# Last stage of a four-layer kernel written in turns: MLP, top-k choice and experts in an order given by hand, with more of the work on ScalarE

## The chip, the core and the metric

The kernel runs on one core of a Trainium2 chip. A core has engines that each work through their own queue of instructions in order: TensorE (PE in the profile; its weight loads are PEld), VectorE (DVE), ScalarE (ACT), GpSimd (POOL), and SyncE (SP), which issues the DMA transfers here. Semaphores make an instruction wait for another engine's result. Matrix products go into PSUM, eight banks of 128 partitions by 512 floats; everything else lies in SBUF. The metric is the device time of one execution in microseconds (us).

## The reference

Eight blocks follow one another, each as `x = x + layernorm(block(layernorm(x)))`, on x of 16 sequences, 256 positions and 128 features in float32. The change lies in the last pieces of this. The seventh block ends in an MLP with a square (all names as in the reference):

```
xa = xa + a_mlp_scale * (square(relu(rms_norm(xa) @ a_fc_w)) @ a_proj_w)
x  = x + layernorm(xa)
```

The eighth block is a mixture of experts in which each of 8 experts chooses its tokens in each sequence. The reference takes k = 2 * t / 8 tokens, which is 64 of 256:

```
probs = softmax(x @ gate_w)                # per token, over 8 experts
g, m  = top_k(probs transposed, k)         # per expert, its 64 tokens
xin   = x[m]
h     = gelu(xin @ w1) @ w2                # 128 -> 512 -> 128, an expert each
out   = zeros.at[m].add(g * h)             # then to bfloat16
x     = x + layernorm(out)
```

## The kernel before, in words

The 16 sequences are kept as 8 groups g of two (`NG`); a group is a tile of 128 partitions by 4 x 128 floats (`NT` = 4 blocks of tokens). `program` runs the stages one after the other. Each stage opens its own pool of working tiles and its own split of the PSUM banks (`LAST_BANKS`: six banks "s" and two "sum" in the last one). A tile asked for under a tag takes the next of that tag's buffers (`bufs`) and waits until the earlier content has been read.

Stages are written as Python generators. A generator emits some instructions and yields. `turns` takes a list of (start turn, generator) and, turn by turn, advances each generator that has begun by one step, in the order of the list; one that is late may make up to three steps. Thus the order in which the source emits instructions is that of the turns. In the stages ahead of the last one `turns` runs inside `k.tc.manual_schedule()`, and each engine's queue then has just this order. In `stage_last` it does not: there the framework's planner sets each engine's order, from its own estimates of durations and with the order of the source as priority.

The last stage (`stage_last`) has three kinds of generators.

`last(g)`, for each group: the MLP in `l3_mlp`, the residual in `residual`, then `choice_gate`. In the MLP, POOL squares the input (L290), VectorE sums (L292), POOL takes the power -1/2 (L245), VectorE multiplies (L298), TensorE transposes (L306) and a copy brings the result to SBUF as `nT`. Four matmuls with `afc` give the hidden layer; ScalarE does relu (L1438) and VectorE multiplies relu by the PSUM value, which is the square (L1439). Sixteen matmuls with `aproj` follow, and VectorE adds to xm (L1444). All matmuls go through the helper at L317. A layer norm is `stats` (VectorE L255 and L257, POOL L244 and L245) and `normed` (four VectorE instructions, L264). `choice_gate` norms x into `xn` (tile name exn), transposes it, multiplies by the gate's weights and takes the softmax over 8 experts into `probs`.

`selection(q)`, for each of four quarters q of four sequences: 32 rows (4 sequences by 8 experts) of 256 probabilities; eight rounds of `max` and `match_replace` on VectorE mark the 64 largest, and three small matmuls rank them into slot numbers.

`pair_of(q, pair)`, 16 of these: for two experts and four sequences, VectorE builds one-hot matrices (`hot`) and POOL the same weighted by the probability (`back`). TensorE gathers the tokens with `hot` into one bank (`xin`), transposes `back` (L1730) into `put`, runs the two experts' w1 and w2, and adds the result back to token positions through `put` into the two banks `sums`. After the fourth pair of a quarter the sums are normed, added to x and stored by DMA.

`copy` at L237 and L239 is a helper that gives every second copy to VectorE and every other to ScalarE. The start turns before are these:

```
    items = [(2 * g if g < 6 else 4 * g - 8, last(g)) for g in range(NG)]
    for q in range(4):
        items.append(((15, 19, 23, 36)[q], selection(q)))
        items += [(21 + 12 * q + 3 * pair, pair_of(q, pair)) for pair in range(4)]
```

The weights of the experts and the gate are issued on SP when the previous stage has ended, 17 transfers that follow one another.

## Time and profile before

| | us |
|---|---|
| median of 3 runs | 3017.48 (3016.08 to 3022.56) |
| the profiled execution, its own time | 3016.38 |
| its span, first to last instruction | 3014.7 |
| busy in the span: TensorE, VectorE, ScalarE, POOL | 2753.9, 1999.3, 1607.1, 1010.7 |
| first instruction of the last stage (POOL, L290, group 0) | starts 2685.78 |
| last matmul of the last stage | ends 3002.76 |

Times inside the profile count from the start of the span. A line of a group has the source line, the engine, the operation, output and inputs with partitions x elements, and how often; then busy time in us and the mean of one in ns; then the engine's idle time just before and which instruction ended it. A float32 matmul of the source appears as two records. A line of a stretch has the start and end, the length, the busy time of each engine with its number of instructions, then the clock that was granted to TensorE (1.00 is full), the DMA share and GB/s. A line of a wait has the waiting engine and tile, the releaser, the total in us, how often, and the longest. A line of the chain has the start, the length and the work. Matmul ends are modelled and overlap the next one's start a little, so lengths of matmul groups are read here from start to start.

### The profile page before, as it was taken

What the parts mean: (1) busy time and instruction counts of PE and PEld (TensorE: products, weight loads), DVE (VectorE), ACT (ScalarE), POOL (GpSimd) and SP (SyncE); (2) the same over time, 40 slices, a digit from 0 to 9 for tenths busy, and PEclk for the clock granted to TensorE, in tenths of its full rate; (3) what the DMA queues carried; (4) which work ended last, traced back from release to release, by engine and by line L of the source; (5) the groups of instructions that cost most, each with busy time, mean ns of one, the idle gap of its engine ahead of it and who ended that gap; (6) DMA issues with size and microseconds to landing.
All of it is one profiled execution on the core that took longest, in us unless ns stands there. A gap on an engine that the chain in (4) does not pass through costs nothing.

```text
span 3014.7 us, 59480 instructions
## 1 busy us (share of the span) xinstructions
PE 2753.9 (91%) x23674; PEld 1882.7 (62%) x23674; DVE 1999.3 (66%) x5462; ACT 1607.1 (53%) x3376; POOL 1010.7 (34%) x1368
## 2 busy tenths in 40 slices
PE   8979999999997799999959997899999699978898
PEld 4647766777666588888743443566666344436897
DVE  5667465574657989999776774565765577638542
ACT  6745556555563567767615665344443377642332
POOL 3553333333335100000044554322222466553332
PEclk9989999999998899999979998899999799988999
DMA  4000000000000000000110000000000000010000
GB/s 114 11 1 2 1 2 2 1 2 1 2 5 33 1 16 8 8 8 8 31 50 1 1 1 1 1 1 1 1 1 2 1 1 1 1 57 1 1 15 15
DMA packets 29150, 31.30 MB, mean 10 GB/s; under 512 B 7292, under 2 KB 20156, under 8 KB 28732
## 3 DMA queue, kind: packets, MB, share of 16 engines
q1 hardware_dynamic: 28872, 27.49, 3.1%
q8 instruction: 187, 3.06, 0.4%
q14 instruction: 91, 0.75, 0.1%
HBM read 23.29 MB, written 4.19 MB: 9 GB/s over the span
## 4 chain that ended last, share of the span: by engine, by line
PE 48%; DVE 9%; ACT 6%; POOL 3%; issue 2%; DMA 0%; POOLq 0%; SPq 0%; ACTq 0%; DVEq 0%
PE ps_s L317 30%; PE ps_o L317 7%; PE ps_mm L317 6%; ACT at_e L472 1%; ACT lg L1129 1%; PE ps_s L306 1%; POOL ln_rs L245 1%; ACT meT L1136 1%; PE ps_sum L317 1%; ACT mdisp L1036 1%; DVE ln_st L255 1%; ACT lg L1009 1%; PE ps_s L506 1%; PE ps_t L1134 1%; DVE at_nm L440 1%
## 5 line engine op out<-in xcount | busy, mean ns | idle before, releaser
L244 POOL TENSOR_SCALAR ln_rs<-ln_mv 128x4 f32<-128x4 f32 x192 | 40.2, 209 | 849.5 <-DVE ln_mv L257 827.8
L440 DVE TENSOR_REDUCE at_nm<-ps_s 128x2 f32<-128x512 f32 (+1 forms) x384 | 238.0, 681 | 122.3 <-PE ps_s L317 122.3
L472 ACT ACTIVATE at_e<-ps_s 128x512 f32<-128x512 f32 x384 | 198.1, 604 | 92.5 <-PE ps_s L317 90.3
L1391 DVE TENSOR_TENSOR scan<-ps_s,lm 128x384 f32<-128x384 f32 x256 | 124.6, 548 | 143.3 <-PE ps_s L317 143.0
L478 POOL TENSOR_SCALAR_AFFINE_SELECT at_e<-at_e 128x1024 f32<-128x1024 f32 (+1 forms) x96 | 135.1, 1408 | 215.5 <-ACT at_e L472 215.2
L245 POOL TENSOR_TENSOR ln_rs<-ln_rs,mhalf 128x4 f32<-128x4 f32 x192 | 196.0, 1021 | 15.7
L854 DVE TENSOR_REDUCE l_max<-ps_s 128x3 f32<-128x384 f32 x256 | 124.0, 547 | 64.1 <-PE ps_s L317 64.1
L317 PE MATMUL ps_o<-my,meT 128*128 128x129 f32 x1024 | 144.4, 288 | 18.8 <-ACT mgot L1148 16.1
L317 PEld LDWEIGHTS ps_s<-l_w,mlp_h 128*128 128x128 f32 x1280 | 149.4, 192 | 19.0 <-issue 15.3
L317 PE MATMUL ps_s<-l1f_phi,mxT 128*128 128x256 f32 x512 | 141.5, 399 | 16.8 <-DVE mpart L1010 16.8
L317 PEld LDWEIGHTS ps_o<-my,meT 128*128 128x128 f32 x1024 | 128.0, 195 | 37.0 <-ACT mgot L1148 22.5
L317 PE MATMUL ps_s<-km,qT 32*128 32x512 f32 x768 | 139.8, 659 | 11.9 <-POOL km L364 10.5
L317 PE MATMUL ps_s<-l_w,mlp_h 128*128 128x128 f32 x1280 | 150.2, 275 | 0.3
L317 PE MATMUL ps_s<-qm,kT 32*128 32x512 f32 x768 | 143.8, 655 | 5.2 <-DVE at_nm L440 5.0
L904 POOL TENSOR_SCALAR_AFFINE_SELECT e<-e 128x512 f32<-128x512 f32 x128 | 78.5, 634 | 178.5 <-ACT e L901 178.5
L317 PE MATMUL ps_o<-at_e,at_vm 128*32 128x128 f32 (+1 forms) x2048 | 122.7, 336 | 15.2 <-ACT at_oT L502 15.2
L317 PE MATMUL ps_mm<-mdisp,mxn 128*128 128x128 f32 x1024 | 125.3, 279 | 5.0 <-DVE mdisp L1048 4.9
L901 ACT ACTIVATE e<-ps_s 128x384 f32<-128x384 f32 x256 | 105.6, 513 | 39.7 <-PE ps_s L317 39.6
L317 PEld LDWEIGHTS ps_mm<-mdisp,mxn 128*128 128x128 f32 x1024 | 121.8, 195 | 7.9 <-DVE mdisp L1048 6.6
L317 PE MATMUL ps_s<-xT,l_w 128*128 128x512 f32 x256 | 119.3, 596 | 2.7 <-ACT mlp_h L789 2.7
L1368 ACT COPY BT<-ps_s 128x512 f32<-128x512 f32 x64 | 37.5, 586 | 154.6 <-PE ps_s L317 154.6
L317 PEld LDWEIGHTS <-b_ident 128*128 128x128 bf16 x656 | 51.4, 98 | 109.3 <-issue 99.5
(427 smaller groups left out, 7098.4 us busy)
## 6 DMA issues: line engine op xcount, KB each, us to landing
mw<-in_l1fw SPq DMA_DIRECT2D x16, 256.0 KB, 2.7
moe_w<-in_moe SPq DMA_DIRECT2D x16, 256.0 KB, 5.3
l_w<-in_l SPq DMA_DIRECT2D x10, 256.0 KB, 3.3
x<-in_x SPq DMA_DIRECT2D x8, 256.0 KB, 4.3
xs<-x SPq DMA_DIRECT2D x8, 256.0 KB, 2.0
slT<-xs SPq DMA_DIRECT2D x8, 256.0 KB, 2.8
out<-x SPq DMA_DIRECT2D x8, 256.0 KB, 2.3
l1f_phi<-in_l1f SPq DMA_DIRECT2D x1, 1024.0 KB, 4.9
```

The costliest lines, as they stand in the source:

```text
L244: g.tensor_scalar(out, in_, scale, eps, ALU.mult, ALU.add)
L245: g.tensor_tensor(out, out, self.mhalf[:, :n], ALU.pow)
L255: v.bn_stats(out=st[:, k, :], in_=src[:, k, :])
L317: self.nc.tensor.matmul(out, lhsT=lhsT, rhs=rhs, start=start, stop=stop, skip_group_check=True)
L440: v_.tensor_reduce(nm[:, t, r, vs], s, AX.X, ALU.max, negate=True)
L472: nc.scalar.activation(e[:, r], s, AF.Exp)
L478: nc.gpsimd.affine_select(at, at, [[0, 4], [0, n], [1, P]], ALU.is_ge, 0.0, base=0, channel_multiplier=-1)
L854: v.tensor_reduce(mx[:, b, :, h, 16], s, AX.X, ALU.max, negate=True)
L901: nc.scalar.activation(e[:, h].rearrange("p j n -> p (j n)"), s[:, : 3 * P], AF.Exp)
L904: nc.gpsimd.affine_select(e[:, :, j, :], e[:, :, j, :], [[0, 4], [1, P]], ALU.is_ge, 0.0, base=0, channel_multiplier=-1)
L1368: nc.scalar.copy(s, ps)
L1391: v.tensor_tensor(m, s[:, : SEQ + P], lm[:, SCAN_HEADS[4 * (t // 2) + 2 * i + hh], :], ALU.mult)
```

## The change

The last stage is put inside `manual_schedule`, with new start turns: the MLP and gate of groups 0 to 5 start at turns 0, 1, 3, 5, 7 and 9, those of groups 6 and 7 at 19 and 21; the selections at 19, 25, 33 and 42; and a pair of experts starts at every second turn from 25. In the list the latest pairs come first, then the selections, then the groups.

`l3_mlp` and `choice_gate` go; their work is written out in `last(g)`, cut into more steps with idle turns after the statistics. The square is a second ScalarE activation in place of VectorE's multiply. All copies out of PSUM are ScalarE's, with one more of them for the MLP's result, which is then added in SBUF. The norm into `xn` is done by four ScalarE activations with scale and bias; POOL makes the bias. The probabilities are written by VectorE without POOL's copies.

In `pair_of` the one-hot matrices are built in twos, a step ahead of their use; the gathered tokens have a PSUM bank of their own ("xin", so five remain for "s"); two sequences' transposed `back` share one bank and one copy of 512 columns. At the end of a quarter both halves are copied and both have their statistics taken before either is normed. More buffers are given to `hot`, `back` and `mlp_h`.

```diff
@@ -32,7 +32,7 @@
 BANKS = {"mm": 2, "s": 2, "o": 2, "t": 2}
 MAMBA_BANKS = {"s": 6, "o": 2, "mm": "s", "t": "s"}
-LAST_BANKS = {"s": 6, "sum": 2, "mm": "s", "t": "s"}
+LAST_BANKS = {"s": 5, "sum": 2, "xin": 1, "mm": "s", "t": "s"}
 ONE_RING = {"s": 8, "mm": "s", "t": "s"}
 RING_BANKS = {"s": 7, "o": 1, "mm": "s", "t": "s"}
 NEG = -(2.0**100)
@@ -1424,26 +1424,6 @@
-def l3_mlp(k, x, fc, proj, bufs=3):
...
@@ -1630,32 +1610,6 @@
-def choice_gate(k, x, g, w, xn, probs):
...
@@ -1667,12 +1621,78 @@
     iota = k.c["iota"].rearrange("p (e c) -> p e c", e=2)
     slots, sums = {}, {}
+    def normed(out, src, mv, rs):
+
+        nb = k.t([P, NT], "ln_nb", 3)
+        nc.gpsimd.tensor_scalar(nb, mv[:, :, 0], -1.0, None, ALU.mult)
+        nc.gpsimd.tensor_tensor(nb, nb, rs, ALU.mult)
+        yield from idle(2)
+        for t in range(NT):
+            nc.scalar.activation(
+                out[:, t, :], src[:, t, :], AF.Identity, bias=nb[:, t : t + 1], scale=rs[:, t : t + 1]
+            )
+
     def last(g):
-        yield from l3_mlp(k, xm[g], w["afc"], w["aproj"], 2)
-        yield
-        yield from k.residual(x[g], xm[g])
-        yield
-        yield from choice_gate(k, x, g, w, xn, probs)
+        xg = xm[g]
+        sq = k.t([P, NT, D], "rms_sq", 2)
+        nc.gpsimd.tensor_tensor(sq, xg, xg, ALU.mult)
+        yield
+        ss = k.t([P, NT], "rms_ss", 3)
+        v.tensor_reduce(ss, sq, AX.X, ALU.add)
+        rs = k.t([P, NT], "rms_rs", 3)
+        k.rsqrt(rs, ss, 1.0 / D, RMS_EPS)
+        yield from idle(2)
+        n = k.t([P, NT, D], "n", 2)
+        v.tensor_tensor(n, xg, bc(rs, 2, D), ALU.mult)
+        yield
+        ps = k.transposed_ps(n)
+        nT = k.t([P, GT], "nT", 2)
+        nc.scalar.copy(nT, ps)
+        yield
+        h = k.t([P, 4, GT], "mlp_h", 4)
+        for i in range(4):
+            ps = k.ps("s")
+            k.mm(ps, w["afc"][:, i * P : (i + 1) * P], nT)
+            nc.scalar.activation(h[:, i, :], ps, AF.Relu)
+            nc.scalar.activation(h[:, i, :], h[:, i, :], AF.Square)
+            if i % 2:
+                yield
+        ps = k.tokens_ps(h, w["aproj"].rearrange("p (c n) -> p c n", c=4))
+        y = k.t([P, NT, D], "ln_y", 3)
+        nc.scalar.copy(y, ps)
+        yield
+        v.tensor_tensor(y, y, xg, ALU.add)
+        mv, rs = k.stats(y)
+        yield from idle(2)
+        k.normed(y, y, mv, rs)
+        nc.gpsimd.tensor_tensor(x[g], x[g], y, ALU.add)
+        yield
+        mv, rs = k.stats(x[g])
+        yield from normed(xn[g], x[g], mv, rs)
+        yield
+        ps = k.transposed_ps(xn[g])
+        xT = k.t([P, GT], "xT", 2)
+        nc.scalar.copy(xT, ps)
+        yield
+
+
+        ps = k.ps("s")
+        for t in range(NT):
+            k.mm(ps[:, t * ne : (t + 1) * ne], xT[:, t * P : (t + 1) * P], w["gate"])
+        p = k.t([P, NT, ne], "p", 3)
+        nc.scalar.copy(p, ps[:, : NT * ne].rearrange("p (t e) -> p t e", t=NT))
+        yield
+        m = k.t([P, NT], "pm", 3)
+        v.tensor_reduce(m, p, AX.X, ALU.max)
+        v.tensor_tensor(p, p, bc(m, 2, ne), ALU.subtract)
+        nc.scalar.activation(p, p, AF.Exp)
+        yield
+        v.tensor_reduce(m, p, AX.X, ALU.add)
+        v.reciprocal(m, m)
+        for b in range(2):
+            at, ts = (2 * g + b) * ne, slice(2 * b, 2 * b + 2)
+            v.tensor_tensor(probs[:, :, at : at + ne], p[:, ts, :], bc(m[:, ts], 2, ne), ALU.mult)
+        yield
     def selection(q):
@@ -1681,22 +1701,25 @@
         for t in range(2):
             nc.tensor.transpose(ps[:rows, t * P : (t + 1) * P], probs[:, t, rows * q : rows * (q + 1)], ident)
         cur = k.t([rows, SEQ], "top", 2)
-        v.tensor_copy(cur, ps[:rows, :SEQ])
+        nc.scalar.copy(cur, ps[:rows, :SEQ])
+        yield
         for n in range(cap // 8):
             best = k.t([rows, 8], "best", 2)
             v.max(out=best, in_=cur)
             nxt = k.t([rows, SEQ], "top", 2)
             v.match_replace(out=nxt, in_to_replace=best, in_values=cur, imm_value=-1.0)
             cur = nxt
-            if n % 2:
+            if n in (2, 5):
                 yield
         chosen = k.t([rows, SEQ], "chosen", 1)
         v.tensor_scalar(chosen, cur, 0.0, None, ALU.is_lt)
+        yield
         ps = k.ps("s")
         for t in range(2):
             nc.tensor.transpose(ps[:, t * rows : (t + 1) * rows], chosen[:, t * P : (t + 1) * P], ident[:rows, :rows])
         mk = k.t([P, 2, rows], "mk", 2)
-        v.tensor_copy(mk, ps[:, : 2 * rows].rearrange("p (t r) -> p t r", t=2))
+        nc.scalar.copy(mk, ps[:, : 2 * rows].rearrange("p (t r) -> p t r", t=2))
+        yield
         rank = k.ps("s")[:, : 2 * rows].rearrange("p (t r) -> p t r", t=2)
         k.mm(rank[:, 0, :], k.c["before"], mk[:, 0, :])
@@ -1709,31 +1732,41 @@
     def pair_of(q, pair):
-        put = k.t([P, nb, SEQ], "put", 4)
-        y = k.t([P, nb, D], "ey", 3)
-        xinT = k.t([P, nb, P], "xinT", 2)
-        xin = k.ps("s").rearrange("p (b c) -> p b c", b=nb)
-        for i in range(nb):
+        def one_hot(i):
             b, r = nb * q + i, i * ne + 2 * pair
-            hot = k.t([P, 2, P], "hot", 4)
+            hot = k.t([P, 2, P], "hot", 6)
             by_expert = hot.rearrange("p t (e c) -> p t e c", e=2)
             v.tensor_tensor(by_expert, bc(iota, 1, 2), bc(slots[q][:, :, r : r + 2], 3, cap), ALU.is_equal)
-            back = k.t([P, 2, P], "back", 4)
+
+            back = k.t([P, 2, P], "back", 6)
             at = b * ne + 2 * pair
             nc.gpsimd.tensor_tensor(
                 back.rearrange("p t (e c) -> p t e c", e=2), by_expert, bc(probs[:, :, at : at + 2], 3, cap), ALU.mult
             )
-            for t in range(2):
-                k.mm(xin[:, i, :], xn[b // 2][:, 2 * (b % 2) + t, :], hot[:, t, :], t == 0, t == 1)
+            return hot, back
+
+        hots = [one_hot(i) for i in range(2)]
+        yield
+        put = k.t([P, nb, SEQ], "put", 4)
+        xin = k.ps("xin").rearrange("p (b c) -> p b c", b=nb)
+        for u in range(2):
+            for i in (2 * u, 2 * u + 1):
+                b = nb * q + i
+                for t in range(2):
+                    k.mm(xin[:, i, :], xn[b // 2][:, 2 * (b % 2) + t, :], hots[i][0][:, t, :], t == 0, t == 1)
             tp = k.ps("s")
-            for t in range(2):
-                nc.tensor.transpose(tp[:, t * P : (t + 1) * P], back[:, t, :], ident)
-            k.copy(put[:, i, :], tp[:, :SEQ])
-            if i % 2:
+            for i in (2 * u, 2 * u + 1):
+                for t in range(2):
+                    at = SEQ * (i % 2) + t * P
+                    nc.tensor.transpose(tp[:, at : at + P], hots[i][1][:, t, :], ident)
+            nc.scalar.copy(put[:, 2 * u : 2 * u + 2, :], tp.rearrange("p (b n) -> p b n", b=2))
+            if u == 0:
+                hots += [one_hot(i) for i in (2, 3)]
                 yield
-        k.copy(xinT, xin)
-        yield
-        h = k.t([P, 2, 4, SEQ], "mlp_h", 3)
+        xinT = k.t([P, nb, P], "xinT", 2)
+        nc.scalar.copy(xinT, xin)
+        yield
+        h = k.t([P, 2, 4, SEQ], "mlp_h", 4)
         for j in range(2):
             w1 = w[f"w1_{2 * pair + j}"]
             for f in (0, 2):
@@ -1752,7 +1785,8 @@
                     rows = slice(j * cap, (j + 1) * cap)
                     w2 = w[f"w2_{2 * pair + j}"].rearrange("p (c n) -> p c n", c=4)
                     k.mm(ps[rows, i, :], h[:, j, f, i * cap : (i + 1) * cap], w2[:, f, :], f == 0, f == 3)
-        k.copy(y, ps)
+        y = k.t([P, nb, D], "ey", 3)
+        nc.scalar.copy(y, ps)
         yield
         if pair == 0:
@@ -1763,19 +1797,28 @@
                 k.mm(o[:, n, :], put[:, i, t * P : (t + 1) * P], y[:, i, :], pair == 0 and n == 0, pair == 3)
         if pair < 3:
             return
-        for u, o in enumerate(sums[q]):
+        obs = []
+        for o in sums[q]:
+            obs.append(k.t([P, NT, D], "ob", 3, dt=BF16))
+            nc.scalar.copy(obs[-1], o)
+        yield
+        got = [k.stats(ob) for ob in obs]
+        yield from idle(2)
+        for u, ob in enumerate(obs):
             g = 2 * q + u
-            ob = k.t([P, NT, D], "ob", 3, dt=BF16)
-            nc.scalar.copy(ob, o)
-            yield
-            yield from k.residual(x[g], ob)
+            n = k.t([P, NT, D], "ln_y", 3)
+            k.normed(n, ob, *got[u])
+            nc.gpsimd.tensor_tensor(x[g], x[g], n, ALU.add)
             nc.sync.dma_start(out=out[2 * g : 2 * g + 2].rearrange("b (t p) d -> p (b t) d", p=P), in_=x[g])
-
-    items = [(2 * g if g < 6 else 4 * g - 8, last(g)) for g in range(NG)]
+        yield
+
+    items = []
     for q in range(4):
-        items.append(((15, 19, 23, 36)[q], selection(q)))
-        items += [(21 + 12 * q + 3 * pair, pair_of(q, pair)) for pair in range(4)]
-    k.turns(items)
+        items += [(25 + 8 * q + 2 * pair, pair_of(q, pair)) for pair in range(4)]
+    items = items[::-1] + [((19, 25, 33, 42)[q], selection(q)) for q in range(4)]
+    items += [((0, 1, 3, 5, 7, 9, 19, 21)[g], last(g)) for g in range(NG)]
+    with k.tc.manual_schedule():
+        k.turns(items)
 @with_exitstack
```

## Prediction

> **What bounds the kernel now.** I read four views, in this order. First the busy times of the whole span, then the span cut into stretches of 10 us from where the last stage begins (its first instruction, the square of group 0 on POOL, starts at 2685.78 us).
>
> ```profile
> PE 2753.9 (91%) x23674; PEld 1882.7 (62%) x23674; DVE 1999.3 (66%) x5462; ACT 1607.1 (53%) x3376; POOL 1010.7 (34%) x1368
> ```
>
> ```profile
> core 0: us, PE busy (x) PEld busy (x) DVE busy (x) ACT busy (x) POOL busy (x), PEclk, DMA share, GB/s
> ...
> 2690.00:2700.00 10.00, 4.01 (x8) 2.06 (x9) 4.53 (x8) 0.60 (x1) 7.28 (x9) 0.50 0.93 341
> ...
> 2730.00:2740.00 10.00, 9.91 (x60) 7.28 (x59) 8.85 (x33) 3.57 (x6) 4.05 (x5) 1.00 0.00 0
> ...
> 2760.00:2770.00 10.00, 5.70 (x14) 2.75 (x14) 8.82 (x47) 1.56 (x4) 4.10 (x8) 0.54 0.00 1
> ...
> 2790.00:2800.00 10.00, 5.91 (x28) 4.46 (x27) 9.04 (x34) 2.85 (x4) 4.25 (x6) 0.83 0.00 1
> ...
> 2810.00:2820.00 10.00, 5.83 (x66) 5.21 (x63) 6.87 (x27) 1.55 (x2) 5.90 (x7) 0.85 0.00 0
> ...
> 2940.00:2950.00 10.00, 10.00 (x108) 9.41 (x105) 2.51 (x6) 2.75 (x5) 2.03 (x4) 1.00 0.01 2
> ```
>
> The reader sees three parts. At the head TensorE waits. From 2750 to 2820 TensorE is 60 to 100% busy at a lowered clock while VectorE is at 90%: that part is VectorE's. After 2820 TensorE is full at clock 1.00: that part is TensorE's. The waits of TensorE in the stage name what was late, and the chain gives the period of the full part.
>
> ```profile
> PE ps_s L306 <- DVE n L298: 7.0, 1, 7.0
> PE ps_s L1697 <- DVE chosen L1694: 6.9, 2, 3.8
> PE ps_s L317 <- DVE nT L237: 6.6, 3, 5.3
> PE ps_s L306 <- DVE exn L264: 4.3, 2, 4.2
> PE ps_sum L317 <- DVE ey L237: 4.2, 1, 4.2
> PE ps_s L317 <- DVE mlp_h L1439: 3.6, 4, 1.8
> ```
>
> ```profile
> 2921.01 1.78 PE ps_sum L317 x16
> ...
> 2932.74 1.78 PE ps_sum L317 x16
> ...
> 2944.48 1.78 PE ps_sum L317 x16
> ```
>
> The six waits all end with VectorE and sum to 32.6 us; a pair of experts costs TensorE 11.74 us (2932.74 - 2921.01, 2944.48 - 2932.74), without a gap.
>
> **TensorE's work, the same before and after.** From the timeline: 4 transposes 0.44 us; the 8 records of afc 3.43 (6 from 2710.43 to 2713.00); the 32 of aproj 3.58 (26 from 2707.52 to 2710.43); so 7.45 a group, and 0.44 + 0.81 more for the transposes and the gate. A selection is about 1.1. Sum: 8 x 8.70 + 4 x 1.1 + 16 x 11.74 = 261.8 us. TensorE works from 2690.73 to 3002.76, which is 312.0. So 50 us are waiting or low clock: the most that an order can give.
>
> **The head.** The stage can't start before POOL's last addition into xm (ends 2685.71), nor do the 16 weight loads move: SP issues them at 2686.1 to 2695.1 either way, and none is read before the first gate. Square, sum, rsqrt and n of group 0 go as before, but n stands behind group 1's sum on VectorE: transposes at 2691.5 instead of 2690.73. The copy of nT goes to ScalarE, which idles 14.9 us here, instead of behind group 2's n on VectorE (the wait of 5.3 above): afc starts at 2693.3 instead of 2697.10.
>
> **Six groups' MLP.** Groups start two turns apart, so on TensorE the order is afc 0-1, afc 2-3 and next group's transposes, aproj. Relu and square now both stand on ScalarE. The nearest rows are the same two lines in an earlier stage, and the norm that has the new form:
>
> ```profile
> L1470 ACT ACTIVATE mlp_h<-mlp_h 128x512 f32<-128x512 f32 x32 | 20.2, 630 | 1.0
> L583 ACT ACTIVATE xn<-x,ln_nb,ln_rs 128x128 f32<-128x128 f32 x32 | 13.1, 483 | 0.0
> L264 DVE TENSOR_SCALAR exn<-x,ln_mv,ln_rs 128x128 f32<-128x128 f32 x32 | 10.5, 361 | 2.8 <-POOL ln_rs L245 2.7
> ```
>
> Four pairs of relu and square take 4 x 1.17 = 4.7 us (2035.46 to 2037.87 is two pairs). They start 1.1 after afc does (0.86 for a matmul, the rest handover), so the last square is done at 5.9; then 2.9 of aproj are left (the other 0.7 can run earlier). Period 8.8 us, of which TensorE works 7.45: **a new stall of 1.35 us a group, on ScalarE**. Queued behind the squares is the next nT copy, which has 2.9 us of aproj as cover. From the cold head: aproj of group 0 ends at 2704.0, of 1 at 2710.4 (its first half overlaps group 0), of 2 and 3 at 2719.2 and 2728.0. In turn 13 group 0's norm (4 x 0.41 = 1.6) stands ahead of group 4's last squares: 2738.4, with one gap of 3.5 us. Group 5 loses 0.8 to two copies and ends at 2748. Before, six groups ended at 2755.6 (timeline): 7.6 earlier.
>
> *Against it* speaks the Trainium skill, ScalarE: Activation LUTs, section Rules for kernel authors: relu and multiply belong on VectorE. In the rows the norm is indeed dearer on ScalarE (483 to 361 ns), the square is not (630 against 676 for the multiply that goes). By the rule, with the multiply on VectorE, the chain would be about 4 x 0.6 + 0.7 = 3.1 us and the stall would go: 6 x 1.35 = 8 us better. I keep the rows' 4.7.
>
> What VectorE loses: per group four multiplies (2.7) and a norm (1.4), and the copies of put (13.1), xinT (9.6), nT, xT, ey, top and mk (9.3): 65 us of its 173. ScalarE's 95 become about 160 in 290 us. Copies of forms not in the trace (128x32, 32x256 on ScalarE) lie between 0.23 (the exp of 128x32) and 0.37 (a copy of 128x256); they lie beside other work except in the selection. Exps of groups 6 and 7 still fall among gelus: table loads stay at 5 of 1.28. POOL gets two small operations for the bias (0.43 a group, rows of the first stage) with two idle turns as cover; it loses two copies.
>
> **The selection.** Group 1's probabilities follow group 5's stats on VectorE: 0.7 copy, 0.6 add, 1.1 stats, 0.5: 2751. Transposes, ScalarE's copy (behind a norm), then 0.4 + 1.05 of other VectorE work: rounds begin at 2753.5. Eight rounds at 0.74 (0.34 + 0.07 + 0.33 start to start) are 5.9, plus 0.27 and 2.5 of other groups' work queued between (probabilities, stats, a sum): 2762.2. Transposes, copy and rank at low clock: **2764.5**, against 2777.5 before. Meanwhile TensorE has 5 us of work, so some 11 us stay idle; behind rank in its queue stand gate 5, afc 6 and all pairs.
>
> **From there TensorE decides.** Left are gate 5, afc 6, transposes 7, aproj 6, group 7 and their gates: 17.8; three selections 3.3; pairs 187.8: 208.9. A two-turn period of pairs gives TensorE 11.74 and ScalarE 4.8 (two copies of put and one each of xinT and ey at 0.59, four gelus at 0.60), the one xin bank is freed by a copy with 3.5 us of w1 and sums as cover, and seven takings of the five s banks always come back after a copy of the turn before: I cost these at nothing; uncovered, a wait of this kind is 0.73 (the ey copy at 3000.07) a pair, 11.7 in all. Restart at low clock: 8 us of half speed (2775.4 to 2784 show it), 4.0. Waits for squares 6 and the last ey: 2.0. End of TensorE 2764.5 + 214.9 = 2979.4, against 3002.76: **23.4 us**.
>
> **The tail.** Before, group 15's half waits: VectorE norms the first half before finishing the second's stats (second half's x at 3011.41, 8.65 after TensorE). Now both stats come first: ob copy 0.62, stats to 1.9, rsqrts back to back to 3.55, norm 1.1, then the second add at 4.85 to 6.1. Gain **2.5**.
>
> **The clock in the six groups** is the unknown. The Trainium skill, TensorE: Matmul & The Clock Gate, Part 1, has the clock halve only after an idle window of about 3.4 us; stalls of 1.35 would then be free. The trace differs: after gaps of 1.17 and 0.30 us the stretch 2725.20 to 2728.00 ran at 0.50, losing 1.4; after gaps of 1.76 and 0.33 it stayed 1.00. One of two, so six stalls cost 3 x 1.4 = 4.2; nothing by the rule; at most, if all six groups ran cold, afc 6.86 and aproj 7.16 give a period of 14 instead of 8.8, 31 us. I take 4.
>
> Sum: 23.4 + 2.5 - 4 = 21.9. The profiled execution took 3016.4 (its span is 3014.7); the median of the runs is 3017.5, 1.1 above. Forecast 3017.5 - 21.9 = **2995.5 us**.
>
> **The rivals.** (1) As worked, 0.55; own range 2986 to 3004 (clock cost 0 to 9, bubble 5 shorter to 4 longer). (2) Better, 0.20: no clock loss and, since POOL and VectorE contend less, half the bubble: 2995.5 - 4 - 5.5 = 2986. For: the page's rule. Against: the 0.50 stretch. (3) In-order queues stall every pair by one uncovered copy: 2995.5 + 11.7 = 3007; 0.12. For: a planner no longer slips work in; against: ScalarE's 40% load. (4) The bubble only moves: selection ends at 2777.5 again, and the low clock returns: within 0.2%, 3017; 0.06. For: the rounds are the same VectorE chain and TensorE has little ready beside it. (5) Slower, 0.07: the clock never rises in the six groups: + 31 - 4: 3022. It is slower once five of six groups run cold (25.9 / 5.2). For: the 0.50 stretch; against: 2706 to 2721 at 1.00 in the same pattern of afc and aproj.
>
> 0.2% (6 us) is about what a measurement of this kernel can tell from no change. Faster: 0.55 + 0.20 + 0.12 = 0.87; same 0.06; slower 0.07. Range 2981 to 3010: cases 1 to 3, leaving 0.15.
>
> **What would show it.** Afc of group 0 at about 2693; TensorE waiting for the square, some 1.3 us a group; the six aproj done near 2748 to 2752; one hole, before the first rank, around 2750 to 2765; then pairs each 11.74 apart with groups 6 and 7 between, TensorE's end near 2980; 6 us, not 8.7, to the last addition. The prediction is wrong if pairs come wider than 12 us, if clock rows from 2700 to 2748 read below 0.8, or if TensorE waits for other engines' old work, such as a late copy, after 2770.

## The result and the profile after

The changed kernel is faster: 3003.9 us (2995.85 to 3004.74, five runs) against 3018.3 for the kernel before on the same chip, ratio 0.9942, 95% interval 0.9928 to 0.9956. The forecast of 2995.5 has the sign right, and its range holds the time; it is 8.4 us too low. The profiled execution took 3001.28 us (span 2999.6), 15.1 less than the one before.

One thing must be set apart first. In this execution the last stage itself begins later, at POOL's last addition into xm: it ends at 2689.27 us, where it ended at 2685.71 before. What lies ahead of it isn't touched by the change. So all kernels here are compared by the **length of the stage**, from the end of that addition to the end of the span: 3014.7 - 2685.7 = 329.0 before, 2999.6 - 2689.3 = 310.3 after. The stage is 18.7 us shorter, and the ratio says the same (0.0058 x 3018 = 17.5).

The busy times of the whole span after:

```profile
PE 2756.1 (92%) x23674; PEld 1881.2 (63%) x23674; DVE 1950.2 (65%) x5342; ACT 1661.9 (55%) x3488; POOL 1017.0 (34%) x1368
```

Three of the stretches of 10 us shown for before, on the changed kernel; they start 3.6 us earlier in the stage than those of before do:

```profile
core 0: us, PE busy (x) PEld busy (x) DVE busy (x) ACT busy (x) POOL busy (x), PEclk, DMA share, GB/s
...
2760.00:2770.00 10.00, 3.63 (x13) 2.64 (x13) 9.49 (x39) 2.60 (x8) 7.00 (x12) 0.50 0.00 1
...
2790.00:2800.00 10.00, 10.00 (x71) 8.59 (x70) 6.57 (x24) 8.05 (x14) 5.10 (x7) 1.00 0.00 0
...
2810.00:2820.00 10.00, 10.00 (x87) 9.14 (x84) 5.96 (x30) 4.54 (x8) 6.72 (x11) 1.00 0.01 2
```

Before, TensorE was 59% busy from 2790 to 2800 and 58% from 2810 to 2820; now it is full in both, at clock 1.00. What is left behind the head is mainly one hole, from 2760 to 2770, where TensorE is 36% busy at clock 0.50 with VectorE at 95% beside it. The waits of TensorE in the stage, and from the chain the line that stands once in each pair of experts, as before:

```profile
PE ps_s L306 <- POOL rms_rs L244: 7.7, 1, 7.7
PE ps_s L317 <- ACT xT L1675: 7.0, 3, 5.4
PE ps_s L317 <- ACT mlp_h L1657: 3.3, 7, 0.7
...
PE ps_sum L317 <- ACT ey L1789: 0.7, 1, 0.7
```

```profile
2924.95 1.78 PE ps_sum L317 x16
...
2936.69 1.78 PE ps_sum L317 x16
```

The first wait is the head; it is 6.8 to 7.7 us in every run here. The waits for VectorE of 4 to 7 us (chosen, nT, exn, ey) no longer stand in the list. The squares cost 3.3 us in seven waits. The hole shows as a wait for xT, 5.4 us in one piece, put down to ScalarE's copy; what that copy waited for is VectorE after all, as shown further down. A pair still takes 11.74 us (2936.69 - 2924.95).

### The profile page after: what moved, and what is told of

Same layout as the page of the kernel before. It is cut to its first block, busy times and chain, and to the rows that moved or that the text cites. A ratio compares the mean times of both kernels' runs of the same rounds, so it can differ in the third digit from the quotient of the medians.

```text
span 2999.6 us, 59389 instructions
## 1 busy us (share of the span) xinstructions
PE 2756.1 (92%) x23674; PEld 1881.2 (63%) x23674; DVE 1950.2 (65%) x5342; ACT 1661.9 (55%) x3488; POOL 1017.0 (34%) x1368
## 4 chain that ended last, share of the span: by engine, by line
PE 51%; ACT 7%; DVE 6%; POOL 2%; issue 2%; DMA 0%; POOLq 0%; SPq 0%; ACTq 0%; DVEq 0%
PE ps_s L317 32%; PE ps_o L317 7%; PE ps_mm L317 6%; ACT at_e L472 1%; PE ps_s L306 1%; ACT lg L1129 1%; PE ps_xin L317 1%; ACT meT L1136 1%; PE ps_sum L317 1%; ACT mdisp L1036 1%; ACT lg L1009 1%; PE ps_s L506 1%; PE ps_t L1134 1%; DVE at_nm L440 1%; POOL ln_rs L245 1%
## 5 line engine op out<-in xcount | busy, mean ns | idle before, releaser
L472 ACT ACTIVATE at_e<-ps_s 128x512 f32<-128x512 f32 x384 | 198.2, 603 | 93.3 <-PE ps_s L317 91.1
L317 PEld LDWEIGHTS ps_s<-l_w,mlp_h 128*128 128x128 f32 x1280 | 149.4, 192 | 18.8 <-issue 15.1
```

The lines of the kernel that those rows point to most:

```text
L317: self.nc.tensor.matmul(out, lhsT=lhsT, rhs=rhs, start=start, stop=stop, skip_group_check=True)
L472: nc.scalar.activation(e[:, r], s, AF.Exp)
```

## The experiments

All kernels here compute the whole reference. Each row is read as above: the stage, the end of TensorE's last instruction and the moment at which VectorE begins to write the first selection's slots (its rank is there then), both counted from the start of the stage, and the ratio to the kernel before.

| run | edit | stage, us | TensorE ends | first slots | ratio (95%) |
|---|---|---|---|---|---|
| before | | 329.0 | 317.1 | 91.8 | 1 |
| after | all | 310.3 | 299.9 | 86.9 | 0.9942 (0.9928 to 0.9956) |
| e1_planner | after, the planner orders it | 304.7 | 294.3 | 81.0 | 0.9925 (0.9911 to 0.9940) |
| e2_order_alone | before, in the order of the source | 402.4 | 390.5 | 114.7 | 1.0254 (1.0236 to 1.0271) |
| e3_vector_square | after, square on VectorE | 321.2 | 311.0 | 95.7 | 0.9975 (0.9966 to 0.9984) |
| e4_early67 | after, groups 6, 7 start earlier | 305.2 | 294.9 | 88.0 | 0.9920 (0.9905 to 0.9935) |
| e5_before_square | before, square on ScalarE | 329.3 | 317.4 | 95.5 | 0.9999 (0.9990 to 1.0008) |
| e6_before_copies | before, copies on ScalarE | 322.4 | 310.5 | 90.9 | 0.9983 (0.9973 to 0.9992) |
| e7_before_both | before, both | 319.1 | 307.1 | 85.7 | 0.9967 (0.9954 to 0.9980) |
| e8_planner_early | e1 and e4 together | 302.1 | 291.8 | 84.5 | 0.9912 (0.9895 to 0.9928) |
| e9_new_starts | e7 and the new start turns | 318.5 | 306.6 | 91.1 | 0.9966 (0.9952 to 0.9980) |
| e10_vector_norm | after, norm into xn on VectorE | 307.9 | 297.6 | 84.1 | 0.9926 (0.9912 to 0.9941) |
| e11_vector_small | after, two small copies on VectorE | 308.2 | 297.8 | 84.5 | 0.9929 (0.9914 to 0.9943) |
| e12_old_front | e1, front of the pairs as before | 303.6 | 293.3 | 80.3 | 0.9924 (0.9906 to 0.9942) |

The stage comes from one profiled execution of each kernel, the ratio from all its runs; what they say of the time agrees within 3.3 us in every row.

### Is it the order, or the new pieces? (e1, e2)

The change has two halves: the last stage in the order of the source, and new pieces to be ordered. e1 keeps the pieces and leaves the order to the planner, as before:

```diff
-    with k.tc.manual_schedule():
-        k.turns(items)
+    k.turns(items)
```

> The changed kernel with its new pieces and start turns, but without manual_schedule in the last stage: the planner orders it again. I call stage length the time from the end of POOL's last addition into xm to the end of the span: 329.0 us before, 310.3 in the changed kernel. Theory 'order': most of the 18.7 us come from the order that is kept, so the planner gives 3012 to 3020 us, stage length 320 to 330, with waits of TensorE for VectorE again between the selections. Rival 'offload': they come from the 65 us of work that VectorE loses, and the planner does as well with it: 3000 to 3006, stage length about 310.

e2 does the reverse to the kernel before: its own pieces and start turns, under the fixed order.

```diff
-    k.turns(items)
+    with k.tc.manual_schedule():
+        k.turns(items)
```

> The kernel before, with its old pieces and old start turns, only put inside manual_schedule in the last stage. Theory 'pieces': the order of the source pays only with pieces that are cut for it; the old ones put a statistic and its use, or a copy and its reader, in one turn, so TensorE waits in its queue at each: 3030 to 3070 us, stage length 340 or more. Rival 'order alone': even so the order keeps the selections from being stretched by other work on VectorE: 3004 to 3012, stage length 312 to 320.

The fixed order earns nothing: theory 'order' is refuted, and the planner did better even than the rival said (about 310). With the new pieces the planner's stage is 304.7 us, 5.6 shorter than the fixed order's, of which some 2 are clock (see e11 below); the intervals of the ratios overlap. TensorE's timeline of e1 in the six groups (start, duration, instruction; idle before and its releaser in brackets) shows what the planner can do that the list can't:

```profile
2719.31 1.12 PE L317 MATMUL ps_s<-nT,l_afc 128*128 128x512 f32 x2 [0.47 <-ACT nT L1650]
2720.28 3.06 PE L317 MATMUL ps_s<-l_aproj,mlp_h 128*128 128x128 f32 x26
...
2728.62 3.06 PE L317 MATMUL ps_s<-l_aproj,mlp_h 128*128 128x128 f32 x26
```

It slips the next group's first two afc records in ahead of an aproj that would wait for a square. Groups come 8.34 us apart (2728.62 - 2720.28) instead of 8.82, and of the seven waits for a square one is left, of 1.1 us. And under the fixed order the old pieces lose 73.4 us, more than the theory 'pieces' had put. The waits of TensorE in e2:

```profile
PE ps_s L306 <- DVE n L298: 25.8, 8, 6.8
PE ps_s L317 <- DVE hot L1720: 16.9, 12, 2.7
PE ps_sum L317 <- ACT ey L239: 10.2, 14, 0.7
PE ps_s L1730 <- POOL back L1723: 8.9, 8, 1.4
```

These four make 61.8 us (before, the wait for n was 7.0, once). In the old front of the pairs hot and back are issued in the turn of their reader, and under the fixed order TensorE waits for them twenty times, 25.8 us in all; n and ey stand one turn ahead of theirs and are still not early enough. The new pieces have hot and back a turn ahead and two idle turns before n; the fixed order needs that and doesn't supply it.

### What the square on ScalarE is worth (e3)

```diff
-            nc.scalar.activation(h[:, i, :], ps, AF.Relu)
-            nc.scalar.activation(h[:, i, :], h[:, i, :], AF.Square)
+            r = k.t([P, GT], "mlp_r", 2)
+            nc.scalar.activation(r, ps, AF.Relu)
+            v.tensor_tensor(h[:, i, :], ps, r, ALU.mult)
```

> The changed kernel with the square again as VectorE's multiply of relu and the PSUM value (tile mlp_r, two buffers), all else as it is. Theory 'ScalarE chain': four relu and square pairs on one engine set the period of 8.82 us a group (aproj ends 2715.64, 2724.46, 2733.29) against 7.45 of TensorE's work; with two engines the period falls to about 7.5 and six groups end 6 to 8 us earlier: stage length 302 to 306. Rival 'VectorE queue': the multiply waits behind older groups' statistics and norms in VectorE's order, the period stays 8.5 or more, and VectorE's 21 us more delay the selection: stage length 310 to 318.

The stage is 10.9 us longer than the changed kernel's, more than either theory gave, and the intervals of the two ratios lie apart. On TensorE in e3, two of the six groups, and the stretch behind the second (its length, busy time and count of each engine, granted clock, DMA):

```profile
2716.98 5.22 PE L317 MATMUL ps_s<-l_aproj,mlp_h 128*128 128x128 f32 x28 [1.79 <-DVE mlp_h L1658]
...
2730.98 5.06 PE L317 MATMUL ps_s<-l_aproj,mlp_h 128*128 128x128 f32 x28 [3.88 <-DVE mlp_h L1658]
```

```profile
2731.00:2735.90 4.90, 4.90 (x29) 4.80 (x30) 1.57 (x9) 0.00 (x0) 2.84 (x7) 0.66 0.00 0
```

The multiply isn't slow; it is late. On VectorE it stands in line behind sums, stats and norms of other groups, so aproj waits up to 3.88 us where it waited 0.66 (in all 8.9 us in six waits, against 3.3 in seven), and after such a wait the granted clock is 0.66: 28 records take 5.06 us, where 26 take 3.17 in the changed kernel.

### The pieces one at a time, on the kernel before (e5, e6, e7, e9)

e5, in the MLP of the kernel before:

```diff
-        r = k.t([P, GT], "mlp_r", bufs)
-        k.nc.scalar.activation(r, ps, AF.Relu)
-        k.nc.vector.tensor_tensor(h[:, i, :], ps, r, ALU.mult)
+        k.nc.scalar.activation(h[:, i, :], ps, AF.Relu)
+        k.nc.scalar.activation(h[:, i, :], h[:, i, :], AF.Square)
```

> The kernel before, planner and old start turns kept, with one edit: the square in the last stage's MLP is ScalarE's activation, in place of VectorE's multiply (21.6 us of VectorE's time). Stage length was 329.0 before, 310.3 in the changed kernel, 304.7 with the changed pieces under the planner, 321.2 with the changed order and VectorE's multiply. Theory 'offload' (formed after those runs: relief of VectorE gives the gain, the kept order costs 5.6): stage length 316 to 323, about half of the 24.3. Rival 'cut': the gain is from the new cut of the pieces and the new start turns, the square alone gives less than 3: stage length 326 to 330.

e6, the helper's copies out of PSUM, and the two written out in the selection:

```diff
+    k.copy = nc.scalar.copy
...
-        v.tensor_copy(cur, ps[:rows, :SEQ])
+        nc.scalar.copy(cur, ps[:rows, :SEQ])
...
-        v.tensor_copy(mk, ps[:, : 2 * rows].rearrange("p (t r) -> p t r", t=2))
+        nc.scalar.copy(mk, ps[:, : 2 * rows].rearrange("p (t r) -> p t r", t=2))
```

> The kernel before, planner and old start turns kept, with all copies out of PSUM in the last stage on ScalarE (put, xinT, nT, xT, ey, and the selection's two), which takes some 32 us from VectorE. Theory 'offload': the waits of TensorE for nT and ey at VectorE (6.6 and 4.2 us in the waits of before) go and the stretch 2750 to 2820 is shorter: stage length 316 to 323. Rival 'cut': less than 3 us, since the selection's rounds on VectorE remain the last to end: 326 to 330.

> The kernel before, planner and old start turns kept, with both edits: squares and all copies out of PSUM on ScalarE. What it lacks against the changed pieces under the planner (304.7) are the norm on ScalarE, the new cut and the new start turns. Theory 'offload': 305 to 311, nearly all of the 24.3. Rival 'cut': 318 to 326, so that the new cut and starts are worth 13 or more.

The square alone is worth nothing under the planner (329.3), the copies alone 6.6, both 9.9: rival 'cut' in e5 and e7, theory 'offload' in e6. That the square is worth nothing in one and 11 us in the other shows how far the price of a piece hangs on the order around it. TensorE's longest wait in e5, and the first two in e7:

```profile
PE ps_s L317 <- DVE nT L237: 13.0, 5, 5.3
```

```profile
PE ps_s L1697 <- DVE pm L1647: 6.5, 1, 6.5
PE ps_s L317 <- ACT mk L1699: 4.8, 4, 3.4
```

In e5 the copy of nT, still on VectorE, is what is late; with both moved, what is left is in the selection. e9 gives e7 the changed kernel's start turns and order of items as well:

```diff
-    items = [(2 * g if g < 6 else 4 * g - 8, last(g)) for g in range(NG)]
+    items = []
...
-        items.append(((15, 19, 23, 36)[q], selection(q)))
-        items += [(21 + 12 * q + 3 * pair, pair_of(q, pair)) for pair in range(4)]
+        items += [(25 + 8 * q + 2 * pair, pair_of(q, pair)) for pair in range(4)]
+    items = items[::-1] + [((19, 25, 33, 42)[q], selection(q)) for q in range(4)]
+    items += [((0, 1, 3, 5, 7, 9, 19, 21)[g], last(g)) for g in range(NG)]
```

> The kernel of e7 (old pieces with squares and copies on ScalarE, planner) with the changed kernel's list of start turns and its order in the list. Stage length was 319.1 with the old starts and 304.7 with the new pieces under the planner. Theory 'cut': what the planner may slip in is set by the pieces (pairs' one-hots a step ahead, one copy of put for two sequences, both statistics before the norms, norm on ScalarE), so the starts alone give at most 4: 315 to 320. Rival 'starts': the priorities that the start turns give are what matters, since the pairs then come every two turns and the third and fourth pair no longer wait for late groups: 305 to 310.

0.6 us: with the old pieces, the start turns by themselves are worth nothing. The selection even ends 5.4 us later than in e7, and the time after it is some 6 shorter.

### The hole (e4, e8)

All that is left in TensorE's queue in the hole needs the selection, or an activation of ScalarE that is late (shown under the selection below). Groups 6 and 7 need neither, but start in turns 19 and 21:

```diff
-    items += [((0, 1, 3, 5, 7, 9, 19, 21)[g], last(g)) for g in range(NG)]
+    items += [((0, 1, 3, 5, 7, 9, 13, 17)[g], last(g)) for g in range(NG)]
```

> The changed kernel with groups 6 and 7 started at turns 13 and 17 instead of 19 and 21. TensorE then has their 15 us of MLP while the first selection runs on VectorE. Theory 'hole': TensorE's idle time from 2754 to 2777 (about 9 us of waits, and the low clock after it, 0.50 from 2760 to 2780) is filled and the clock stays up: stage length 298 to 303. Rival 'queues': the squares of groups 6 and 7 stand ahead of the selection's copies on ScalarE and their statistics between its rounds on VectorE, so the selection ends that much later and the hole only moves: stage length 308 to 314.

> The changed pieces under the planner (no manual_schedule), with groups 6 and 7 started at turns 13 and 17. Alone, the planner gave a stage length of 304.7 and the earlier groups 305.2, against 310.3. Theory 'hole': under the planner TensorE still waits 5.5 for the first selection and 3.5 for a norm, and 2750 to 2770 is half empty; groups 6 and 7 fill it: 298 to 302, about 2990 us. Rival 'same time': both edits win the same microseconds, so together 303 to 306, about 2995 us.

e4's stretch over the place of the hole, and the new waits of its TensorE:

```profile
2760.00:2770.00 10.00, 8.13 (x51) 7.14 (x49) 9.52 (x41) 6.57 (x17) 5.25 (x10) 0.83 0.01 2
```

```profile
PE ps_xin L317 <- DVE hot L1739: 2.2, 2, 1.3
...
PE ps_s L1761 <- POOL back L1743: 2.2, 3, 0.9
```

The hole is filled (8.13 us busy instead of 3.63), and the stage is 5.1 shorter, short of the 7 to 12 of the theory 'hole': the first slots come 1.1 us later, and TensorE now waits 4.4 us for hot and back in pairs that start without cover from groups 6 and 7. With the planner as well (e8) the stage is 302.1, at the edge of the forecast 298 to 302, and the ratio 0.9912 is the lowest of the table; its interval touches that of the changed kernel and overlaps those of e1 and e4.

### Norm, small copies, front of the pairs (e10, e11, e12)

```diff
-        yield from normed(xn[g], x[g], mv, rs)
+        yield from idle(2)
+        k.normed(xn[g], x[g], mv, rs)
```

> The changed kernel, its order kept, with the norm into xn again as four VectorE instructions (two idle turns ahead of it stay). Theory 'ScalarE queue': the norm's 1.63 us stand in ScalarE's order ahead of group 4's squares, of the gate's copies and of the selection's mk copy, so without them the six groups end 1.6 earlier and the first rank comes 1 to 3 earlier; VectorE pays 1.1 twice between the selection's rounds. In sum stage length 307 to 311 (310.3 in the changed kernel), no worse on VectorE. Rival 'offload': VectorE is what decides at the selection, and the norm there costs its 1.1 for each of groups 2 to 5: 313 to 316.

```diff
-        nc.scalar.copy(cur, ps[:rows, :SEQ])
+        v.tensor_copy(cur, ps[:rows, :SEQ])
...
-        nc.scalar.copy(mk, ps[:, : 2 * rows].rearrange("p (t r) -> p t r", t=2))
+        v.tensor_copy(mk, ps[:, : 2 * rows].rearrange("p (t r) -> p t r", t=2))
```

> The changed kernel, its order kept, with the selection's two copies (256 columns of top, 64 of mk) on VectorE as before the change. In the changed kernel mk's copy starts at 2773.42, 2.2 us after its transposes were issued, because a norm of group 5 and a gate's copy stand ahead of it on ScalarE. Theory 'ScalarE queue': mk comes about 2 us earlier and the copy of top costs VectorE 0.4: stage length 308 to 309. Rival 'TensorE order': rank stands behind group 5's and 6's transposes on TensorE, which wait for the same norm, so nothing is won: 310 to 312.

Both stages are some 2 us shorter than the changed kernel's (2.4 and 2.1), as the theory 'ScalarE queue' had it in both, and yet in both a difference of this size lies in a part that the edit doesn't touch. The same 15 us in the changed kernel and in e11, as a stretch, then the aproj of group 4 in either; the last number but two of a stretch is the clock:

```profile
2735.00:2750.00 15.00, 13.81 (x67) 9.82 (x65) 6.21 (x37) 12.17 (x26) 5.29 (x9) 0.89 0.00 1
```

```profile
2735.00:2750.00 15.00, 13.81 (x78) 9.59 (x77) 6.79 (x40) 13.68 (x29) 6.07 (x11) 1.00 0.00 1
```

```profile
2740.63 4.75 PE L317 MATMUL ps_s<-l_aproj,mlp_h 128*128 128x128 f32 x26 [0.66 <-ACT mlp_h L1657]
```

```profile
2741.00 3.17 PE L317 MATMUL ps_s<-l_aproj,mlp_h 128*128 128x128 f32 x26 [0.66 <-ACT mlp_h L1657]
```

After the same wait of 0.66 us the same 26 records take 4.75 us in one and 3.17 in the other (3.17 in e10 too): 1.6 us, in a part that e11 doesn't edit. At the head, group 1's afc takes 4.34 us from start to start in the changed kernel and 3.4 in e10 and e11, 0.9 more. Together 2.5, as much as either gain. So the place of the norm and of the small copies is worth about nothing under the fixed order. e11 tests one thing more: whether the rank waited for ScalarE's copy of mk. TensorE from the transposes of chosen to the rank, in the changed kernel and in e11:

```profile
2771.68 0.42 PE L1719 MATMUL ps_s<-const_ident,chosen 32*128 32x32 f32 x2
...
2774.69 0.47 PE L317 MATMUL ps_s<-mk,const_before 128*128 128x32 f32 x2
```

```profile
2770.76 0.42 PE L1719 MATMUL ps_s<-const_ident,chosen 32*128 32x32 f32 x2
...
2773.76 0.47 PE L317 MATMUL ps_s<-mk,const_before 128*128 128x32 f32 x2
```

3.0 us in both: it is TensorE's own order, two other groups' transposes between, and not the copy. The number of the theory 'ScalarE queue' came, its mechanism didn't.

e12 puts the old front of the pairs (one-hot, put, xin in the s banks; the copies stay on ScalarE) into e1:

```diff
-LAST_BANKS = {"s": 5, "sum": 2, "xin": 1, "mm": "s", "t": "s"}
+LAST_BANKS = {"s": 6, "sum": 2, "mm": "s", "t": "s"}
...
-        hots = [one_hot(i) for i in range(2)]
-        yield
...
+        xin = k.ps("s").rearrange("p (b c) -> p b c", b=nb)
+        for i in range(nb):
...
+            k.copy(put[:, i, :], tp[:, :SEQ])
+            if i % 2:
                 yield
```

> The changed pieces under the planner (stage length 304.7), with only the front of the pairs as before the change: each one-hot is built, used and its transposed weights copied (128x256, on ScalarE) one sequence after the other, hot and back have four buffers, and the gathered tokens share the six s banks. Theory 'front': this cut is what lets TensorE run without a wait behind the first selection (one wait of 5.5 for chosen and none after it, against waits of 2.9, 3.0 and 0.6 for put, hot and back with the old front in e9), so it is worth 6 to 10 of the 14.4 us between e7 and e1: stage length 311 to 315. Rival 'groups': the longer cut of the MLP, the gate and the selection is what counts, and the front gives under 3: 303 to 308.

303.6 against 304.7: with the planner the new front is worth nothing, as the rival 'groups' had it. From 2810 to 2980 e12's TensorE has no gap:

```profile
2810.00:2980.00 170.00, 170.00 (x1723) 157.46 (x1723) 60.97 (x188) 81.08 (x162) 45.29 (x67) 1.00 0.04 11
```

**What the runs make of it.** Under the planner the new pieces save 329.0 - 304.7 = 24.3 us. Squares and copies on ScalarE are 9.9 of it, the start turns 0.6, the tail 1.6 (its end behind TensorE 7.1 instead of 8.65), the front of the pairs nothing. If the pieces add up, which the square shows they need not, the remaining 12 lie in how the groups and the selection are newly cut (yields, idle turns, y copied out of PSUM before it is added, norm on ScalarE, probs written without POOL). They come early: e9 and e1 have the same start turns, and e1's first slots are 10.1 us ahead of e9's (81.0 and 91.1), TensorE's end 12.3. The first instruction of the selection's rounds, in e9 (stage from 2691.1) and in e1 (stage from 2689.1), says where:

```profile
2761.36 0.42 DVE L1687 MAX8 best<-top 32x8 f32<-32x256 f32 x1 [2.09 <-ACT top L1684]
```

```profile
2751.64 0.42 DVE L1708 MAX8 best<-top 32x8 f32<-32x256 f32 x1
```

The rounds begin 70.2 us into the stage in e9 and 62.6 in e1. So 7.7 of the 10.1 are won before the rounds, on the way to the first probabilities, nothing in the rounds (0.2 the other way), and 2.6 between chosen and the slots. Which of the cuts it is wasn't separated; the norm was moved back under the fixed order alone (e10). On top of the 24.3 the fixed order costs 5.6 in the profiles, or 0.2% in the ratios, whose intervals leave room for no cost at all.

## Why the prediction was right, and where its sizes were off

All times from the start of the stage; forecast, then measured, in us.

| step | forecast | measured | off by |
|---|---|---|---|
| afc of group 0 starts | 7.6 | 7.5 | -0.1 |
| period of a group | 8.8 | 8.82 | 0 |
| six aproj end (with the 4 for the clock) | 66.3 | 65.5 | -0.8 |
| from there to the end of the rank | 16.5 | 21.1 | +4.6 |
| from there to TensorE's end | 214.9 | 213.4 | -1.5 |
| TensorE's end to the last addition | 6.1 | 7.1 | +1.0 |

Off by 3.3 in all: 21.9 were forecast, 18.7 came (17.5 by the ratio). Of the rest of the 8.4, 3.6 lie ahead of the stage in the profiled execution, and 1.5 between the executions profiled and the medians. The sum is that of the whole change and does not part the order from the pieces: that the planner would make as much or more of the same pieces (e1) was not asked. VectorE's busy time in the stage fell by 49.5 us (178.4 to 128.9) and not by 65, ScalarE's rose by 53.7 (95.5 to 149.2); no term of the sum rests on these.

**The head** came as worked out. TensorE's timeline:

```profile
2696.78 3.78 PE L317 MATMUL ps_s<-nT,l_afc 128*128 128x512 f32 x4 [0.72 <-ACT nT L1650]
```

7.5 us into the stage; before it was 11.4, behind VectorE's copy of nT.

**The stall of the squares** is there in every group, and the period is right because the whole ScalarE chain was counted, not the busy time it adds. The visible wait is smaller than the 1.35 named (aproj waits 0.19 and then 0.66 in a group). The estimate that the rule of the Trainium skill, ScalarE: Activation LUTs, section Rules for kernel authors (multiply on VectorE), would be 8 us better is contradicted by e3: it is 10.9 us worse. The rule compares the engines per element, and here the queue decides.

**The clock** was charged with 4 us, three drops of 1.4. The stretch of three groups, and the one behind it:

```profile
2705.50:2737.00 31.50, 29.27 (x172) 21.38 (x171) 16.69 (x77) 20.15 (x37) 15.92 (x24) 1.00 0.00 1
2737.00:2745.20 8.20, 7.01 (x39) 5.95 (x38) 1.19 (x6) 6.02 (x14) 3.27 (x6) 0.79 0.00 0
```

Three groups with a stall each ran at 1.00, as the Trainium skill, TensorE: Matmul & The Clock Gate, Part 1, has it for gaps far below its idle window of about 3.4 us; then, behind gaps of 0.37 and 0.66 us, came one drop that cost 1.6 us, which that window does not give and which e10 and e11 don't have in the same place. One drop, not three: the charge was 1.5 too high with the head's 0.9 in it. Whether a drop comes varies from execution to execution, so how near this term came is in part luck.

**The selection is the term that was mis-sized**, by 4.6 us. I took a round at 0.74 us, the distances of its three instructions to their next neighbours in the trace of before:

```profile
2763.19 0.41 DVE L1687 MAX8 best<-top 32x8 f32<-32x256 f32 x1
2763.53 0.32 DVE L264 TENSOR_SCALAR exn<-x,ln_mv,ln_rs 128x128 f32<-128x128 f32 x1
2763.77 0.07 DVE L1689 MATCH_VALUE_LOAD top<-best,top 32x8 f32 x1
2763.84 0.40 DVE L1689 MATCH_REPLACE8 top<-best,top 32x256 f32<-32x256 f32 x1
2764.17 0.33 DVE L264 TENSOR_SCALAR exn<-x,ln_mv,ln_rs 128x128 f32<-128x128 f32 x1
```

VectorE's timeline after:

```profile
2760.35 0.41 DVE L1708 MAX8 best<-top 32x8 f32<-32x256 f32 x1
2760.80 0.08 DVE L1710 MATCH_VALUE_LOAD top<-best,top 32x8 f32 x1
2760.88 0.40 DVE L1710 MATCH_REPLACE8 top<-best,top 32x256 f32<-32x256 f32 x1
2761.31 0.42 DVE L1708 MAX8 best<-top 32x8 f32<-32x256 f32 x1
```

0.96 us: each instruction waits for the end of the one whose result it reads. Before, the planner had put an independent instruction (here two of a norm) between MAX8 and the load and another behind the replace, and these covered that time; from the start-to-start times I had read a price that holds only with such company. Eight rounds: +1.8, and some 0.4 more for the other groups' work between them.

From chosen to the rank's end I had 2.3 us; it took 4.7 (2771.2 to 2775.9), the other +2.4. ScalarE, then TensorE:

```profile
2769.12 0.23 ACT L1688 ACTIVATE p<-p 128x32 f32<-128x32 f32 x1 [5.21 <-DVE p L1687]
...
2771.87 1.65 ACT L1631 ACTIVATE exn<-x,ln_nb,ln_rs 128x128 f32<-128x128 f32 x4
...
2773.42 0.19 ACT L1721 COPY mk<-ps_s 128x64 f32<-128x64 f32 x1
```

```profile
2769.88 1.88 PE L317 MATMUL ps_s<-moe_gate,xT 128*128 128x8 f32 x8 [5.44 <-ACT xT L1675]
```

An exp of another group waits 5.21 us for a subtraction that stands among VectorE's rounds. The copy of xT stands behind that exp, the gate that reads xT behind the copy, and the transposes of chosen behind the gate in TensorE's queue: chosen is there at 2771.20, they run at 2771.68, as soon as the gate is through. This is the hole of 5.4 us, and of the +2.4 it makes at most 0.5. Behind them stand two other groups' transposes, which wait 0.32 for a norm and last 2.3 at the low clock (0.50 in this stretch); then comes the rank, at 2774.69. ScalarE's copy of mk, late behind the norm, is hidden beside them, as e11 shows. I had asked what is queued behind the rank, and not what stands ahead of it in each of three queues.

**From there TensorE decides**, as forecast: from 2783.2 to 2989.2 it is busy 205.26 of 206.0 us at clock 1.00, and rival 3 (every pair stalls) is refuted by the 11.74. Its wait for ey comes once, at the end:

```profile
2987.16 2.05 PE L317 MATMUL ps_sum<-ey,put 128*128 128x128 f32 x16 [0.74 <-ACT ey L1789]
...
2991.55 1.12 DVE L264 TENSOR_SCALAR ln_y<-ob,ln_mv,ln_rs 128x128 f32<-128x128 bf16 x4 [0.39 <-POOL ln_rs L245]
...
2992.85 1.26 POOL L1811 TENSOR_TENSOR x<-x,ln_y 128x512 f32<-128x512 f32 x1
2992.92 2.05 DVE L264 TENSOR_SCALAR ln_y<-ob,ln_mv,ln_rs 128x128 f32<-128x128 bf16 x4 [0.25 <-POOL ln_rs L245]
2995.05 1.26 POOL L1811 TENSOR_TENSOR x<-x,ln_y 128x512 f32<-128x512 f32 x1 [0.93 <-DVE ln_y L264]
```

**The tail** gained 1.55 of the 2.5: the second norm, priced at 1.1 like the first, took 2.05. POOL's addition of the first half, which the new order of the tail brings next to it, starts 0.07 us ahead of it. Taken one by one, the norm's first instruction lasts 1.28 us and ends 0.08 after the addition, and the other three last 0.34 each, as they do in the first norm. Before, both norms of the tail took 1.1, with POOL idle beside them. All eight runs with the new tail have the second norm at 2.04 or 2.05 us, the six with the old one at 1.11 or 1.12.

**Of the rivals**, 1 is what came, at the end of its own range (2986 to 3004). Rival 2 (no clock loss, half the bubble, 2986) didn't come, and no kernel here reaches it; e8, with the lowest ratio, has a median of 2994.6. The hole that rival 4 feared came, 5.4 us in one piece, but the rank came some 5 us earlier in the stage than before (first slots at 86.9 and 91.8; 9 had been forecast with the clock's charge), and TensorE ran full behind it. Rival 5 (cold clock) didn't come: 1.00 over three groups. Of the three signs of being wrong none came: the pairs are 11.74 apart, the rows of 10 us from 2700 to 2750 have a clock of 0.83 or more, and behind the hole no wait of TensorE reaches 1 us.

## What to carry to other kernels

A fixed order earns its keep only when it beats the planner on the same pieces, so run the pieces under both: here the gain was in the pieces, and the order added nothing to it. Where order is fixed, a reader belongs a turn behind its producer, and further where the producer itself ends a chain (in e2, with one turn, TensorE still waited 25.8 us for n), and the price of an operation on an engine is its place in that engine's queue before it is its duration. For a step that holds an in-order engine for several us, list what stands ahead of its reader in each queue on the way, and price a chain of dependent instructions end to end, not start to start in a trace where others ran between.

## What the hardware showed that was not expected

- A chain of dependent VectorE instructions of 32x256 (0.41, 0.08 and 0.40 us) takes 0.96 us a round by itself, 0.07 more than its sum; with independent instructions between, the three take 0.74 of VectorE's time.
- A norm of four VectorE instructions of 128x128 from bf16 took 1.12 us beside POOL work of 128x4, and 2.05 when POOL's addition of 128x512 had just begun: the one instruction that starts behind the addition's start lasts until the addition ends (1.28 or 1.29 us instead of 0.34, at three places of the changed kernel). It looks like a full wait and not like a slower instruction; why was not tested.
- The same instructions after the same gap of 0.66 us took 3.17 us in one execution and 4.75 in another (the group of 4.75 lies in a stretch at clock 0.79). By such differences a single profile of this stage is good to some 2.5 us, and smaller differences in the stage's length were not read as effects of an edit.
